# A residual added in SBUF by GpSimd and VectorE instead of by accumulating transfers, at the end of a convolution, attention and recurrence kernel

## The chip, the cores and the metric

The kernel runs on one core of a Trainium2 chip. A core has a matrix engine (TensorE, PE in the profile, with its weight load PEld), three engines for elementwise work (VectorE, DVE; ScalarE, ACT; GpSimd, POOL), an engine that issues transfers (SyncE, SP), and 16 DMA engines which move data between SBUF, the core's memory of 128 partitions, and HBM. PSUM holds the results of matmuls. The metric is device time in microseconds (us) of one execution, as the median of several.

## The reference

The input x has 8 images (B) of 128 channels and 48 x 48 = 2304 tokens. Cut to what matters here:

```python
# layer 0: group norm, then causal attention of each image, added to x
x = x + _L0_conv_ref(_gn(x), Wq, bq, Wk, bk, Wv, bv)
# layer 1
t = _to_tokens(x)
t = t + _L1_attn_ref(_ln_t(t))                      # full attention of the normalized tokens with themselves
t = t + _L1_ffn_ref(_ln_t(t), W, V, gamma, beta)    # the recurrence
x = _from_tokens(t, x)

def _L1_ffn_ref(x, W, V, gamma, beta):
    Wx = jnp.einsum('bti,hi->bth', x, W)
    # ... batch norm of Wx over all images and tokens, gamma and beta
    def step(yt, wx_t):
        yt = jax.nn.sigmoid(wx_t + yt @ V.T)
        return (yt, yt)
    _, ys = jax.lax.scan(step, jnp.zeros((B, H)), jnp.swapaxes(Wx, 0, 1))
    return jnp.swapaxes(ys, 0, 1)
```

The last line of layer 1 matters most: the output is a residual, t after the second attention (t2 in the kernel), plus the states y of the recurrence, for 8 x 2304 tokens of 128 channels: 9.44 MB in fp32.

## The kernel before

The kernel does the two attentions image by image, and keeps W times the normalized tokens in SBUF (wx). When all images are done, and so the statistics of the batch norm are known, the recurrence runs. It isn't done token after token: the 2304 tokens are cut into 96 segments (SEGS) of LS = 24 steps, which run side by side. Each segment begins with 12 warm-up steps (WARM) on the tokens before it. At the end, the last state of each segment is compared with the warmed-up state of the next; a flag says whether they differ too much, and a general path, which isn't taken here, would then compute all again. The 96 segments are in three groups of 32 (SG), so that a step is three matmuls of 256 columns (8 images x 32 segments), one for each group; while one group is in ScalarE another is in TensorE.

The residual is written to the output as soon as the attention has it, group by group of segments:

```python
def keep():                                   # for each image b and chunk j of 384 tokens
    tp = transposed(c["t2"], f"tk_{b}_{j}")
    g, s0 = divmod(j * SJ, SG)
    if s0 == 0:
        self.t2c = work1.tile([P, LS, SG], F32, tag="t2c", name=f"t2c_{b}_{g}")
    nc.scalar.copy(self.t2c[:, :, ds(s0, SJ)], tp[:, :QC].rearrange("p (s l) -> p l s", l=LS))
    if s0 + SJ == SG:
        nc.sync.dma_start(out[g, :, :, b, :], self.t2c)
```

The recurrence adds the states to it with transfers that accumulate, issued by GpSimd, four steps at a time (TO), and two at a time at the end:

```python
WARM = 12
G = SEG_GROUPS                                # 3
TZ = 2
TO = 4
# ... pools: rst[g] with 4 buffers for y, PSUM for z; zeroing of the banks
mv = rc.tile([P, 2], F32, tag="bn_mv", name="bn_mv")
nc.vector.bn_aggr(mv, stats)                  # batch norm: a and c from mv
# ...
def inputs(g, t):                             # z for two steps: SBUF to PSUM, on VectorE
    # ...
    nc.vector.tensor_scalar(z, wx[:, t : t + TZ, :, s0 : s0 + SG], a, c, ALU.mult, ALU.add)
    # ...
for t in range(-WARM, LS):
    s, so = t % TZ, t % TO
    for g in range(G):
        if s == 0 and t + TZ < LS:
            zs[g].append(inputs(g, t + TZ))
        if so == 0:
            y[g] = rst[g].tile([P, TO, B, SG], F32, tag="y", name=f"y_{g}_{t}")
        z = zs[g][0]
        nc.tensor.matmul(z[:, s], vT_f, prev[g], start=False, stop=True, skip_group_check=True)
        to = warm[g] if t == -1 else y[g][:, so]
        nc.scalar.activation(to, z[:, s], AF.Sigmoid)
        prev[g] = to
        # ...
        if so == TO - 1 and 0 <= t < LS - 1:
            nc.gpsimd.dma_start(out[g, :, t + 1 - TO : t + 1], y[g], accum_op=ALU.add)
        if t >= LS - TO and s == TZ - 1:
            nc.gpsimd.dma_start(out[g, :, t + 1 - TZ : t + 1], y[g][:, so + 1 - TZ : so + 1], accum_op=ALU.add)

d = rc.tile([P, G, B, SG], F32, tag="d", name="d")
dm = rc.tile([P, G], F32, tag="dm", name="dm")
for g in range(G):                            # the seams between segments
    n = SG if g < G - 1 else SG - 1
    nc.vector.tensor_sub(d[:, g, :, : SG - 1], prev[g][:, :, : SG - 1], warm[g][:, :, 1:])
    if n == SG:
        nc.vector.tensor_sub(d[:, g, :, SG - 1 :], prev[g][:, :, SG - 1 :], warm[g + 1][:, :, 0:1])
    nc.vector.tensor_reduce(dm[:, g : g + 1], d[:, g, :, :n], AX.XY, ALU.max, apply_absolute_value=True)
# ... off from dm, a matmul over the partitions, and the flag
```

After that every engine loads the flag and branches:

```python
redo = nc.values_load(flag[0:1, 0:1], min_val=0, max_val=1, ...)     # L1359
with tc.If(redo > 0):                                                # L1360
    general_path(tc, *args)
```

GpSimd has one more task in the attention that is used below: it multiplies 128 x 128 blocks of the probabilities by a triangle of ones (L950), while VectorE adds up the probabilities (L971).

Of the kernel before, what the change touches and what calls it, by code (L numbers as in the profile page):

```python
# [13 lines left out]
F32 = mybir.dt.float32  # L14
AF = mybir.ActivationFunctionType
ALU = mybir.AluOpType
AX = mybir.AxisListType
# [7 lines left out]
SEGS = 96  # L25
SEG_GROUPS = 3
# [574 lines left out]
def fast_path(ctx: ExitStack, tc: tile.TileContext, x, wq, bq, wk, bk, wv, bv, w_ffn, v_ffn, gamma, beta, pe, out, flag):  # L601
    nc = tc.nc
    B, C, H, W = x.shape
    N = H * W
    P = 128
    assert C == P and N % P == 0
    NB = N // P
    CH = 512
# [9 lines left out]
    dpool = ctx.enter_context(tc.tile_pool(name="dram", bufs=1, space=DRAM))  # L618


    LS = N // SEGS
    SG = SEGS // SEG_GROUPS
    SJ = QC // LS
    wx = cpool.tile([P, LS, B, SEGS], F32, tag="wx", name="wx")

    posb_d = dpool.tile([P, NQ, 3, QC], F32, tag="posb_d", name="posb_d")

    ident = cpool.tile([P, P], F32, tag="ident", name="ident")
# [20 lines left out]
    with ExitStack() as actx:  # L649
# [40 lines left out]
        def load_x(b):  # L690
# [12 lines left out]
            out=grp3, in_=grp3, compare_op=ALU.is_ge, fill=0.0, base=0, pattern=[[-cg, GROUPS], [0, cg]], channel_multiplier=1  # L703
        )
        nc.gpsimd.affine_select(
            out=grp3, in_=grp3, compare_op=ALU.is_ge, fill=0.0, base=cg - 1, pattern=[[cg, GROUPS], [0, cg]], channel_multiplier=-1
# [323 lines left out]
        class Full:  # L1030
# [103 lines left out]
            def after(self, j, o):  # L1134
                b, rows, tsum = self.b, self.rows, self.tsum
                cols = ts(j, QC)
                c = {}
                o_sb = chunk_tile("o", f"of_{b}_{j}", c, 2)
                nc.scalar.copy(o_sb, o[:, :QC])
                at = st.then(st.now, [("ACT", 0.5)])  # L1140

                def sums():

                    dn = small.tile([P, QB], F32, tag="dn", name=f"dn_{b}_{j}")
                    nc.vector.tensor_reduce(dn, rows[:, QB * j : QB * (j + 1), : j + 1], AX.X, ALU.add)
                    n = NQ - 1 - j
                    if n:
                        tp = psum_t(f"ts_{b}_{j}")
                        k = n * R * QB
                        nc.tensor.matmul(  # L1150
                            tp[:, :k], same.rearrange("p a c -> p (a c)"), tsum[j][:, :n, :].rearrange("p n k -> p (n k)"),
                            start=True, stop=True,
                        )
                        own = small2.tile([P, NQ - 1, R, QB], F32, tag="own", name=f"own_{b}_{j}")
                        nc.vector.tensor_mul(
                            own[:, :n].rearrange("p n a g -> p (n a g)"), tp[:, :k], mine[:, :n].rearrange("p n a g -> p (n a g)")
                        )
                        more = small.tile([P, QB], F32, tag="more", name=f"more_{b}_{j}")
                        nc.vector.tensor_reduce(more, own[:, :n].rearrange("p n a g -> p g (n a)"), AX.X, ALU.add)
                        nc.vector.tensor_add(dn, dn, more)  # L1160
                    ri = small.tile([P, QB], F32, tag="ri", name=f"ri_{b}_{j}")
                    nc.vector.reciprocal(ri, dn)
                    c["ri"] = ri

                def residual():
                    tp = transposed(o_sb, f"of_t_{b}_{j}")
                    t2 = chunk_tile("t2", f"t2_{b}_{j}", c, 5)
                    for g in range(QB):
                        nc.vector.scalar_tensor_tensor(
                            t2[:, ts(g, P)], tp[:, ts(g, P)], c["ri"][:, g : g + 1], t1_tok[b, j][:, ts(g, P)], ALU.mult, ALU.add  # L1170
                        )
                    c["t2"] = t2
                    c["mv"], c["ve"] = moments(t2, f"f{b}_{j}", "l2")

                def rooted():
                    c["rs"] = root(c["ve"], f"f{b}_{j}", "l2")

                def normed():
                    c["x2"] = chunk_tile("x2", f"x2_{b}_{j}", c, 6)
                    normalize(c["x2"], c["t2"], c["mv"], c["rs"])  # L1180

                def keep():
# [4 lines that stand above are left out]
                        self.t2c = work1.tile([P, LS, SG], F32, tag="t2c", name=f"t2c_{b}_{g}")  # L1187
                    nc.scalar.copy(self.t2c[:, :, ds(s0, SJ)], tp[:, :QC].rearrange("p (s l) -> p l s", l=LS))
                    if s0 + SJ == SG:
                        nc.sync.dma_start(out[g, :, :, b, :], self.t2c)  # L1190

                def back():
                    tp = transposed(c["x2"], f"tx_{b}_{j}")
                    c["xc"] = chunk_tile("xc", f"xc_{b}_{j}", c, 7, bufs=1)
                    nc.scalar.copy(c["xc"], tp[:, :QC])

                def statistics():
                    tp = psum_t(f"wx_{b}_{j}")
                    nc.tensor.matmul(tp[:, :QC], w1T, c["xc"], start=True, stop=True)  # L1199
                    nc.vector.bn_stats(stats[:, b * NQ + j, :], tp[:, :QC])  # L1200
                    nc.scalar.copy(wx[:, :, b, ts(j, SJ)], tp[:, :QC].rearrange("p (s l) -> p l s", l=LS))

                c["chain"] = st.add([
                    (sums, 0.15, [("DVE", 0.8)]),
                    (residual, 0.35, [("DVE", 2.6)]),
                    (rooted, 0.0, [("POOL", 0.9)]),
                    (keep, 0.35, [("ACT", 0.5)]),
                    (normed, 0.0, [("DVE", 1.1)]),
                    (back, 0.35, [("ACT", 0.5)]),
                    (statistics, QC * US, [("DVE", 0.55), ("ACT", 0.85)]),  # L1210
                ], max(at, st.free["DVE"]) + 0.2 - st.now)
# [37 lines left out]
    WARM = 12  # L1249
    G = SEG_GROUPS  # L1250
    TZ = 2
    TO = 4
    assert LS * SEGS == N and WARM % TZ == 0 and LS % TO == 0 and SG * B * TZ == CH
    with ExitStack() as rctx:
        rc = rctx.enter_context(tc.tile_pool(name="rconst", bufs=1))
        rst = [rctx.enter_context(tc.tile_pool(name=f"rst{g}", bufs=4)) for g in range(G)]
        ps_z = [rctx.enter_context(tc.tile_pool(name=f"ps_z{g}", bufs=2, space=PSUM)) for g in range(G)]
        ps_w = rctx.enter_context(tc.tile_pool(name="ps_w", bufs=1, space=PSUM))

        rctx.enter_context(tc.manual_schedule())  # L1260

        zero = rc.tile([P, CH], mybir.dt.bfloat16, tag="zero", name="zero")
        nc.gpsimd.memset(zero, 0.0)
# [41 lines left out]
        prev, warm, y = [], [], [None] * G  # L1305
        for g in range(G):
# [3 lines left out]
            warm.append(rc.tile([P, B, SG], F32, tag=f"warm_{g}", name=f"warm_{g}"))  # L1310
            zs[g].append(inputs(g, -WARM))

        for t in range(-WARM, LS):
            s, so = t % TZ, t % TO
            for g in range(G):
                if s == 0 and t + TZ < LS:
                    zs[g].append(inputs(g, t + TZ))
                if so == 0:
                    y[g] = rst[g].tile([P, TO, B, SG], F32, tag="y", name=f"y_{g}_{t}")
                z = zs[g][0]  # L1320
                nc.tensor.matmul(z[:, s], vT_f, prev[g], start=False, stop=True, skip_group_check=True)  # L1321
                to = warm[g] if t == -1 else y[g][:, so]
                nc.scalar.activation(to, z[:, s], AF.Sigmoid)
                prev[g] = to
                if t == -1 and g == 0:
                    nc.vector.memset(warm[0][:, :, 0:1], 0.0)
                if s == TZ - 1:
                    zs[g].popleft()

                if so == TO - 1 and 0 <= t < LS - 1:  # L1330
                    nc.gpsimd.dma_start(out[g, :, t + 1 - TO : t + 1], y[g], accum_op=ALU.add)
                if t >= LS - TO and s == TZ - 1:
                    nc.gpsimd.dma_start(out[g, :, t + 1 - TZ : t + 1], y[g][:, so + 1 - TZ : so + 1], accum_op=ALU.add)

        d = rc.tile([P, G, B, SG], F32, tag="d", name="d")
        dm = rc.tile([P, G], F32, tag="dm", name="dm")
        for g in range(G):
            n = SG if g < G - 1 else SG - 1
            nc.vector.tensor_sub(d[:, g, :, : SG - 1], prev[g][:, :, : SG - 1], warm[g][:, :, 1:])
            if n == SG:  # L1340
                nc.vector.tensor_sub(d[:, g, :, SG - 1 :], prev[g][:, :, SG - 1 :], warm[g + 1][:, :, 0:1])
            nc.vector.tensor_reduce(dm[:, g : g + 1], d[:, g, :, :n], AX.XY, ALU.max, apply_absolute_value=True)
        off = rc.tile([P, 1], F32, tag="off", name="off")
        nc.vector.tensor_reduce(off, dm, AX.X, ALU.max)
        nc.vector.tensor_scalar(off, off, STATE_TOL, None, ALU.is_gt)
# [44 lines left out]
```

## Time and profile before

| | |
|---|---|
| median of 3 runs | 1867.28 us (1866.15 to 1867.42) |
| the profiled execution | 1867.69 us, span of the profile 1866.0 us |
| PE busy | 1817.0 us, 97% of the span |
| DVE, ACT, POOL busy | 65%, 41%, 10% |
| transfers issued by SyncE | 188.79 MB |
| transfers issued by GpSimd (the accumulating ones) | 9.44 MB |

The span is the time from the first to the last instruction of the profiled execution. A line such as L1331 is a line of the kernel's source. The lists of instructions give, for a group, the tile written, the tile read, the shape, and busy time and mean duration in ns. An engine that ends with a q (PEq, POOLq, SPq) is that engine's sequencer, which handles waits, branches and transfers. The chain of waits is followed back from the last instruction: at each step it names what released the next. A table by windows gives the busy time of each engine in chosen stretches of the span, with the granted TensorE clock, the mean busy share of the 16 DMA engines and the GB/s they moved. Kinds of transfer are listed with KB each and the median us from issue to landing.

### The profile page before, as it was taken

Reading aid. Unit: us, or ns where it says so; the run is one execution under the profiler, and the core shown is the slowest. Engines: PE = TensorE matmul, PEld = TensorE weight load, DVE = VectorE, ACT = ScalarE, POOL = GpSimd, SP = SyncE. Lnnn points to the kernel's source line nnn. Section 1 sums busy time; section 2 is a strip of 40 time slices with the busy share of each in tenths; the row PEclk is TensorE's granted clock in tenths of the full one; section 3 lists DMA queues with packets and bytes.
Section 4 is the critical chain, followed back from the end, with each engine's and each line's share of the span. In section 5 each row is a group of like instructions: output and inputs, shape, how many; then the busy total and the mean of one; then the engine's idle time right before and its main releaser. Section 6 shows DMA issues by size and latency. Waiting matters only on the chain.

```text
span 1866.0 us, 22237 instructions
## 1 busy us (share of the span) xinstructions
PE 1817.0 (97%) x6885; PEld 1159.3 (62%) x6886; DVE 1212.5 (65%) x3146; ACT 773.6 (41%) x1976; POOL 187.3 (10%) x288
## 2 busy tenths in 40 slices
PE   7999999999999999999999999999999999999984
PEld 4666666666666666666666666666666666666663
DVE  5747667576766667476676767666675766756473
ACT  2345334443344424453344433444244533444353
POOL 1100011000110002000110001100020001100013
PEclk9999999999999999999999999999999999999987
DMA  2105551256204561055512462045610554024619
GB/s 91 51 1 190 158 129 32 92 158 176 70 14 140 162 160 47 3 188 163 128 28 95 155 180 66 13 140 164 157 47 6 185 163 121 9 71 154 173 24 190
DMA packets 173982, 200.43 MB, mean 107 GB/s; under 512 B 85465, under 2 KB 147548, under 8 KB 173854
## 3 DMA queue, kind: packets, MB, share of 16 engines
q1 hardware_dynamic: 169728, 188.79, 35.3%
q0 software_dynamic: 3024, 9.44, 2.7%
q8 instruction: 57, 0.93, 0.2%
q10 hardware_dynamic: 1102, 0.68, 0.2%
q14 instruction: 71, 0.58, 0.1%
HBM read 105.67 MB, written 93.19 MB: 107 GB/s over the span
## 4 chain that ended last, share of the span: by engine, by line
PE 95%; DMA 2%; issue 1%; DVE 1%; ACT 0%; POOL 0%; SPq 0%; POOLq 0%; DVEq 0%
PE s L1114 18%; PE o L1128 17%; PE s L945 16%; PE o L956 16%; PE o L1124 12%; PE pj L850 3%; PE pj L853 2%; PE wx L1199 2%; PE dn L987 1%; PE x_t L908 1%; PE tb L908 1%; DMA out_dram<-y 1%; PE of_t L908 1%; PE tx L908 1%; PE z L1321 1%
## 5 line engine op out<-in xcount | busy, mean ns | idle before, releaser
L1116 ACT ACTIVATE p<-s,shift 128x384 f32<-128x384 f32 x504 | 293.0, 581 | 448.5 <-PE s L1114 435.5
L1114 PE MATMUL s<-xh 128*128 128x384 f32 x1008 | 410.8, 489 | 0.0
L1128 PE MATMUL o<-p,xhT 128*128 128x384 f32 x1008 | 403.2, 487 | 0.0
L945 PE MATMUL s<-q,k 128*128 128x384 f32 (+2 forms) x1008 | 379.7, 458 | 0.5 <-DVE k L860 0.5
L956 PE MATMUL o<-p,vT 128*128 128x384 f32 (+2 forms) x1008 | 376.9, 456 | 0.0
L947 ACT ACTIVATE p<-s 128x384 f32<-128x384 f32 (+2 forms) x504 | 230.9, 462 | 349.5 <-PE s L945 286.5
L1124 PE MATMUL o<-g,xhT 128*128 128x384 f32 x720 | 279.7, 488 | 0.3 <-DMA g<-e 0.3
L1128 PEld LDWEIGHTS o<-p,xhT 128*128 128x128 f32 x1008 | 188.0, 190 | 121.3
L956 PEld LDWEIGHTS o<-p,vT 128*128 128x128 f32 x1008 | 188.5, 190 | 114.4
L1114 PEld LDWEIGHTS s<-xh 128*128 128x128 f32 x1008 | 183.7, 190 | 106.8
L971 DVE TENSOR_TENSOR acc<-acc,p 128x384 f32<-128x384 f32 (+2 forms) x408 | 210.3, 515 | 59.9 <-ACT p L947 38.0
L945 PEld LDWEIGHTS s<-q,k 128*128 128x128 f32 x1008 | 178.3, 191 | 88.8 <-DVE acc L971 1.1
L1077 DVE STREAM_TRANSPOSE t<-p 128x384 f32<-128x384 f32 x360 | 187.0, 553 | 45.1 <-ACT p L1116 42.5
L1124 PEld LDWEIGHTS o<-g,xhT 128*128 128x128 f32 x720 | 132.1, 190 | 79.3 <-issue 1.5
L1087 DVE TENSOR_REDUCE tsum<-t 128x12 f32<-128x1152 f32 x120 | 162.4, 1353 | 4.1
L855 DVE TENSOR_TENSOR z<-pj,pb 128x384 f32<-128x384 f32 x144 | 79.3, 551 | 110.4 <-PE pj L850 105.6
L950 POOL TENSOR_TENSOR p<-p,triu 128x128 f32<-128x128 f32 x144 | 72.2, 502 | 447.4 <-ACT p L947 446.6
L898 POOL TENSOR_TENSOR rs_f<-ve_f,mhalf 128x3 f32<-128x3 f32 x48 | 41.5, 865 | 687.2 <-DVE ve_f L892 687.2
L1116 ACT ACTIVATION_READ_ACCUMULATOR p<-s,shift 128x1 f32 x504 | 97.3, 193 | 0.0
L989 DVE RECIPROCAL ric<-dn 128x3 f32<-128x3 f32 x48 | 8.5, 177 | 135.9 <-PE dn L987 135.9
L999 DVE SCALAR_TENSOR_TENSOR t1t<-oc_t,ric,xr 128x128 f32<-128x128 f32 x144 | 41.6, 345 | 68.3 <-ACT xr L996 67.9
L850 PE MATMUL pj<-xn,wT 128*128 128x384 f32 x192 | 80.7, 506 | 0.0
(236 smaller groups left out, 1570.6 us busy)
## 6 DMA issues: line engine op xcount, KB each, us to landing
e<-t SPq DMA_DIRECT2D x120, 576.0 KB, 3.3
g<-e SPq DMA_DIRECT2D x480, 144.0 KB, 3.8
pb<-posb_d SPq DMA_DIRECT2D x42, 576.0 KB, 4.2
x<-in_x_dram SPq DMA_DIRECT2D x16, 576.0 KB, 4.7
out_dram<-t2c SPq DMA_DIRECT2D x24, 384.0 KB, 4.4
out_dram<-y POOLq DMA_DIRECT2D x15, 512.0 KB, 13.3
posb_d<-pb SPq DMA_DIRECT2D x6, 576.0 KB, 2.8
out_dram<-y POOLq DMA_DIRECT2D x6, 256.0 KB, 16.5
```

Source lines behind the costliest of these rows:

```text
L850: nc.tensor.matmul(ps[:, :QC], wT[:, j, :], xn, start=True, stop=True)
L855: nc.vector.tensor_add(z, ps[:, :QC], c["pb"][:, j, :])
L945: nc.tensor.matmul(s[:, off:QC], keys[b][:, ts(m, P)], queries[b, j][:, off:], start=True, stop=True)
L947: nc.scalar.activation(p[:, off:], s[:, off:QC], AF.Exp, scale=SCALE)
L956: nc.tensor.matmul(o[:, off:QC], vals[b][:, ts(m, P)], p[:, off:], start=first, stop=last)
L971: nc.vector.tensor_add(a[:, off:], a[:, off:], p[:, off:])
L1077: nc.vector.transpose(t[:, :, :, g, :].rearrange("p b j r -> p j b r"), p.rearrange("p (j b r) -> p j b r", j=QB, b=R))
L1087: nc.vector.tensor_reduce(self.tsum[j][:, n - j - 1, :], t.rearrange("p b j m r -> p (b j) (m r)"), AX.X, ALU.add)
L1114: nc.tensor.matmul(s[:, :QC], xh[:, ts(m, P)], xh[:, ts(j, QC)], start=True, stop=True)
L1116: nc.scalar.activation(p, s[:, :QC], AF.Exp, bias=shift, accum_out=self.rows[:, m, j : j + 1])
L1124: nc.tensor.matmul(out_ap, xhT[:, QB * i + g, :], p, start=first, stop=last)
L1128: nc.tensor.matmul(o[:, :QC], xhT[:, what[1], :], p, start=first, stop=last)
```

## The change

Two thirds of the residual, groups 1 and 2, and the last four steps of group 0, no longer go to the output from the attention but to a scratch tensor in HBM (t2_d). Behind the attention they are loaded into SBUF (t2s). In the recurrence they are added there to the states, two steps at a time: by GpSimd up to step 19, by VectorE for the last four steps. SyncE then stores the sums to the output with plain transfers. The first 20 steps of group 0 are accumulated by transfers as before. The y tiles of groups 1 and 2 hold two steps in place of four and have six buffers in place of four, and the comparison of the seams is done for each group as soon as its last step is there. It is meant to replace transfers that accumulate, which read and write the output, by additions in SBUF and plain stores.

```diff
+    t2_d = dpool.tile([SEG_GROUPS, P, LS, B, SG], F32, tag="t2_d", name="t2_d")
+    LM = LS - 4
@@ keep()
-                        nc.sync.dma_start(out[g, :, :, b, :], self.t2c)
+                        n = 0 if g else LM
+                        if n:
+                            nc.sync.dma_start(out[g, :, :n, b, :], self.t2c[:, :n])
+                        nc.sync.dma_start(t2_d[g, :, n:, b, :], self.t2c[:, n:])
@@ the recurrence
-    TO = 4
+    TO = [4] + [2] * (G - 1)
-        rst = [rctx.enter_context(tc.tile_pool(name=f"rst{g}", bufs=4)) for g in range(G)]
+        rst = [rctx.enter_context(tc.tile_pool(name=f"rst{g}", bufs=4 if g == 0 else 6)) for g in range(G)]
+        t2s = [rc.tile([P, LS if g else LS - LM, B, SG], F32, tag=f"t2s_{g}", name=f"t2s_{g}") for g in range(G)]
+        for l in range(0, LS, 8):
+            for g in range(1, G):
+                nc.sync.dma_start(t2s[g][:, l : l + 8], t2_d[g, :, l : l + 8])
+        nc.sync.dma_start(t2s[0], t2_d[0, :, LM:])
+        def seams(g):
+            # ... the body of the loop over the seams, for one group
@@ in the loop over t and g
-                if so == TO - 1 and 0 <= t < LS - 1:
-                    nc.gpsimd.dma_start(out[g, :, t + 1 - TO : t + 1], y[g], accum_op=ALU.add)
-                if t >= LS - TO and s == TZ - 1:
-                    nc.gpsimd.dma_start(out[g, :, t + 1 - TZ : t + 1], y[g][:, so + 1 - TZ : so + 1], accum_op=ALU.add)
                 if s == TZ - 1:
                     zs[g].popleft()
+                    l0 = t + 1 - TZ
+                    if 0 <= l0 and (g or l0 >= LM):
+                        r = t2s[g][:, l0 : l0 + TZ] if g else t2s[0][:, l0 - LM : l0 - LM + TZ]
+                        (nc.gpsimd if l0 < LM else nc.vector).tensor_add(r, y[g][:, so + 1 - TZ : so + 1], r)
+                        nc.sync.dma_start(out[g, :, l0 : l0 + TZ], r)
+                    elif l0 >= 0 and so == TO[0] - 1:
+                        nc.gpsimd.dma_start(out[0, :, t + 1 - TO[0] : t + 1], y[0], accum_op=ALU.add)
+                if t == LS - 1:
+                    seams(g)
```

More of the change, by code (lines that the diff above doesn't have):

```diff
@@ L1251, in fast_path @@
     TZ = 2
-    TO = 4
-    assert LS * SEGS == N and WARM % TZ == 0 and LS % TO == 0 and SG * B * TZ == CH
+    TO = [4] + [2] * (G - 1)
+    assert LS * SEGS == N and WARM % TZ == 0 and LS % TO[0] == 0 and SG * B * TZ == CH
     with ExitStack() as rctx:
         rc = rctx.enter_context(tc.tile_pool(name="rconst", bufs=1))
-        rst = [rctx.enter_context(tc.tile_pool(name=f"rst{g}", bufs=4)) for g in range(G)]
+        rst = [rctx.enter_context(tc.tile_pool(name=f"rst{g}", bufs=4 if g == 0 else 6)) for g in range(G)]
         ps_z = [rctx.enter_context(tc.tile_pool(name=f"ps_z{g}", bufs=2, space=PSUM)) for g in range(G)]
@@ L1311, in fast_path @@
             zs[g].append(inputs(g, -WARM))
+        d = rc.tile([P, G, B, SG], F32, tag="d", name="d")
+        dm = rc.tile([P, G], F32, tag="dm", name="dm")
+        def seams(g):
+            n = SG if g < G - 1 else SG - 1
+            nc.vector.tensor_sub(d[:, g, :, : SG - 1], prev[g][:, :, : SG - 1], warm[g][:, :, 1:])
+            if n == SG:
+                nc.vector.tensor_sub(d[:, g, :, SG - 1 :], prev[g][:, :, SG - 1 :], warm[g + 1][:, :, 0:1])
+            nc.vector.tensor_reduce(dm[:, g : g + 1], d[:, g, :, :n], AX.XY, ALU.max, apply_absolute_value=True)
         for t in range(-WARM, LS):
-            s, so = t % TZ, t % TO
+            s = t % TZ
             for g in range(G):
@@ L1317, in fast_path @@
                     zs[g].append(inputs(g, t + TZ))
+                so = t % TO[g]
                 if so == 0:
-                    y[g] = rst[g].tile([P, TO, B, SG], F32, tag="y", name=f"y_{g}_{t}")
+                    y[g] = rst[g].tile([P, TO[g], B, SG], F32, tag="y", name=f"y_{g}_{t}")
                 z = zs[g][0]
@@ L1328, in fast_path @@
                     zs[g].popleft()
-                if so == TO - 1 and 0 <= t < LS - 1:
-                    nc.gpsimd.dma_start(out[g, :, t + 1 - TO : t + 1], y[g], accum_op=ALU.add)
-                if t >= LS - TO and s == TZ - 1:
[L1333 to L1342, printed above, removed]
+                    l0 = t + 1 - TZ
[7 more added lines that the diff above has]
+                    seams(g)
         off = rc.tile([P, 1], F32, tag="off", name="off")
```

## The prediction

> **What bounds the kernel now.** I read the windows first, because busy shares of the whole span mix two stages. Up to 1776 us TensorE is busy without a break (attention). From 1791 to 1840 us come 36 steps of three groups each, one matmul every 0.43 us in the chain of waits, again at full TensorE. The rest is tail. Columns below: window, its length, then busy us and (instructions) of PE, PEld, DVE, ACT, POOL, then granted clock, DMA share, GB/s.
>
> ```profile
> core 0: us, PE busy (x) PEld busy (x) DVE busy (x) ACT busy (x) POOL busy (x), PEclk, DMA share, GB/s
> 1812.00:1814.00 2.00, 2.00 (x11) 1.76 (x10) 1.65 (x3) 1.76 (x6) 0.37 (x1) 1.00 0.00 0
> 1814.00:1838.00 24.00, 24.00 (x113) 21.11 (x112) 19.52 (x27) 21.34 (x57) 13.06 (x15) 1.00 1.01 190
> 1838.00:1862.40 24.40, 1.84 (x10) 1.21 (x8) 3.00 (x11) 1.89 (x5) 5.19 (x6) 0.59 1.07 203
> ```
>
> The 16 DMA engines are saturated from the first accumulating transfer (1814) to 1862.4: 9.44 MB in 48.4 us, 195 GB/s. TensorE stops at 1840, so 22 us of the tail are transfers alone. The chain of waits, in order of time (start, us, what), and the page's list of transfers (KB each, us to landing) say the same:
>
> ```profile
> 1834.32 16.75 DMA out_dram<-y
> 1851.07 0.02 issue
> 1851.10 0.02 POOLq L1333
> 1851.11 0.48 issue
> 1851.59 0.88 POOLq L1359
> ```
> ```profile
> out_dram<-y POOLq DMA_DIRECT2D x15, 512.0 KB, 13.3
> out_dram<-y POOLq DMA_DIRECT2D x6, 256.0 KB, 16.5
> ```
>
> Under the transfers lies a second floor: the end of the program. The flag is written at 1842.7; each engine then loads it and branches.
>
> ```profile
> L1359 PEldq TENSOR_LOAD <-flag x1: 1771/1771/1771, 1842.7 to 1842.7; - x1
> L1359 POOLq TENSOR_LOAD <-flag x1: 1488/1488/1488, 1851.6 to 1851.6; - x1
> ```
> ```profile
> L1360 PEldq COMPARE_BRANCH  x1: 6777/6777/6777, 1844.6 to 1844.6; - x1
> L1360 POOLq COMPARE_BRANCH  x1: 45/45/45, 1853.1 to 1853.1; - x1
> L1360 POOLq EVENT_SEMAPHORE  x1: 17/17/17, 1859.7 to 1859.7; - x1
> ```
>
> The branch costs 6.8 us on PE (1844.6 to 1851.4) and 6.6 on POOL (1853.1 to 1859.7), which arrives last because its accumulating issues held it until 1851.6. So even with no transfers at all the end would be 1842.7 + 1.8 + 6.8 + about 2 of closing waits = 1853.3: at most 13 us of the 22 can be had.
>
> **What the Trainium skill says.** (1) "GPSIMD Engine Reference", section 3, gives a GpSimd tensor_tensor add over 2048 fp32 as 4497 ns and calls it about twice VectorE's. The trace has GpSimd's 128x128 product at 457 ns median (the mean, 502, holds the delays of (2)); a line through both is 457 + 384 x 2.1 = 1.27 us for 128x512, an estimate; no run here shows that size yet. (2) "SBUF — State Buffer", "Who interferes with whom": a VectorE instruction with two SBUF inputs excludes a GpSimd one that reads SBUF; one with at most one SBUF input outside the 2-port modes doesn't. The trace agrees with the first half: the product doubles beside a VectorE add and is 0.45 us alone.
>
> ```profile
> 44.10 0.91 POOL L950 TENSOR_TENSOR p<-p,triu 128x128 f32<-128x128 f32 x1 [2.24 <-ACT p L947]
> 44.15 0.55 DVE L971 TENSOR_TENSOR acc<-acc,p 128x384 f32<-128x384 f32 x1
> ...
> 45.96 0.45 POOL L950 TENSOR_TENSOR p<-p,triu 128x128 f32<-128x128 f32 x1 [0.95 <-ACT p L947]
> ```
>
> (3) "VectorE: DVE Perf Modes", "Why PSUM operands drop a tier": with a PSUM operand the 2-port mode is out. The recurrence's z (SBUF to PSUM, 0.81 us each) should so leave GpSimd alone; GpSimd reads no SBUF operand beside it in this trace, so that isn't shown. (4) "DMA: Bandwidth & Descriptors", "Measured", gives 341 GB/s for a 1 MB load; in the trace the first load of x (4.6 KB pieces) runs at 417 GB/s, in the window from 4 to 6 us.
>
> **The change, part by part.**
> Attention: the instruction order on PE, DVE and ACT is the same but for buffer names up to the recurrence, and GpSimd and SyncE differ only in where t2c is stored: 24 stores become 32 of the same bytes. 0 us.
>
> Loads: 6 of 1.05 MB and one of 0.52 MB, 6.8 MB, in 8 KB pieces. In the built program the first waits for the last use of the attention's tiles (the residual, 1779.2 us) and the others for the last store of t2c (issued 1780.1, landed about 1785). At 340 to 417 GB/s the remaining 5.8 MB need 14 to 17 us: done by 1803. The first add comes at step 1, about 1811.4. The DMA is idle from 1784 to 1814 now, so this is hidden: 0 us.
>
> GpSimd in the recurrence: two steps last 6 x 0.432 = 2.59 us. Per two steps it now has 2 adds of 1.27 and half an accumulating issue of 0.88: 2.98 us. It falls behind by 0.4 us each time. From 1811.4: 20 x 1.27 + 5 x 0.88 + 1 us of gaps = 30.8, so it would end at 1842.2, against 1835 if it kept up. Ring: y of groups 1 and 2 has 6 buffers of two steps, so a step waits for the add of twelve steps before; that bites only above about 4.3 us per two steps. The recurrence stays at TensorE's pace and still ends at 1840.2.
>
> VectorE at the end: six adds at 0.68 us (558 ns for 384 elements in the trace, 325 for 128: 0.9 per element), 4.1 us, and the seam checks, which moved among them. Without interference: first adds at 1836.8, then the last group's step at 1840.2, flag at about 1845.3 (1842.7 before). But GpSimd is adding until after 1842, and two-input adds exclude one another: four GpSimd adds (5.1 us) interleave with VectorE's. I take a third to a half of that on VectorE's chain: flag 1847; GpSimd, delayed by three VectorE adds, ends about 1845.
>
> Transfers: the accumulating ones fall from 9.44 MB to 2.62 MB (13 us at 205 GB/s), the plain stores are 6.8 MB (20 us at 340). 33 us of work lie between 1813 and 1850, so there's no long backlog. SyncE stores in order: the last six stores stand behind GpSimd's last add (1845); 8 x 0.26 MB at 340 GB/s are 6 us, landing 2 us later: 1853.
>
> Sum: flag 1847 + load 1.8 + branch 5 to 6.8 (the branch was timed while the DMA was saturated; I don't know how much of it that is) + 2 of closing = 1856 to 1857.6. The transfers' 1853 and their wait of 1.7 us at the end are just below. Span 1856.7; the median before is 1.3 us above its span: **1858 us**, 9.3 us less, half a per cent.
>
> **The rivals.**
> GpSimd becomes the bound. If an add costs 1.9 us instead of 1.27, GpSimd ends at 1811.4 + 38 + 5.4 = 1854.8, then 1.5 + 6.6 + 1.5 for its flag, branch and close: 1864.4, or 1866 as a time, nearly nothing gained. For it: the average of the 144 products is 502 ns, above the median, and GpSimd is already short of time by my sum. Against: 4497 ns for 2048 elements leaves little room.
>
> z and GpSimd exclude each other after all. Then per two steps 2.43 us of z and 2.54 + 0.44 of GpSimd are in series, 5.4 us in place of 2.59, and the recurrence's last 24 steps take 65 us instead of 31: about 1890. Against: the issues of accumulating transfers (2.6 us for three) cost as much beside z as after it. They don't read SBUF operands, so this is weak evidence, but with (3) I give it 4 in 100.
>
> The exclusion at the end costs nothing and the branch shrinks once the DMA is quiet: flag 1845.3 + 1.8 + 4 + 2 = 1853, time 1854. For it: the page shows DMA share 1.07 during PE's branch. One in five.
>
> Stores slower than thought: at 210 GB/s (as the accumulating ones) the last stores end at 1857 and set the end, 1860.
>
> **Range and chances.** The floor of 1853 forbids 2% (37 us) of gain, unless the branch vanished; only the second rival makes 2% of loss. The middle cases lie between 1854 and 1866. Range 1850 to 1866; faster 0.01, same 0.96, slower 0.03.
>
> **What would show it.** Right: loads landed before 1806; GpSimd's adds near 1.27 us and busy almost without gaps from 1811 to 1845; PE busy until 1840; in the chain of waits the end belongs to the flag and the branch, not to out_dram<-y; DMA share well under 1 after 1850. Wrong: adds of 1.9 us or more, ACT waiting for GpSimd's adds in the recurrence, z above 0.81 us, VectorE adds longer than 0.7 us by waiting (then the exclusion is larger than I took), or a last store that lands after the branch.

## The result and the profile after

| | before | after |
|---|---|---|
| median | 1867.35 us (1866.15 to 1869.34) | **1855.2 us** (1853.79 to 1856.92) |
| ratio, 95% interval | | 0.9934 [0.9917, 0.9952] |
| the profile's span | 1866.0 us | 1852.4 us |
| start of the last recurrence matmul | 1839.3 us | 1838.6 us |
| from there to the end (the tail) | 26.7 us | 13.8 us |

The change takes 12 us, two thirds of a per cent. From execution to execution the mean granted clock differs in the third digit (0.986 to 0.995 in these runs), and the end of the attention moves with it by several us. So where a few us matter, I read each profile from the start of TensorE's last recurrence matmul on. That stretch is called the tail below.

First the windows of the changed kernel, with the columns of the prediction's windows:

```profile
1796.00:1800.00 4.00, 4.00 (x21) 3.51 (x20) 3.86 (x7) 3.57 (x10) 0.00 (x0) 1.00 1.01 426
1800.00:1804.00 4.00, 4.00 (x20) 3.54 (x19) 3.91 (x7) 3.56 (x10) 0.00 (x0) 1.00 0.33 129
...
1814.00:1838.00 24.00, 24.00 (x113) 20.91 (x112) 20.86 (x28) 21.26 (x56) 24.00 (x23) 1.00 1.03 262
...
1844.00:1846.00 2.00, 0.19 (x2) 0.09 (x2) 1.61 (x6) 0.00 (x0) 0.00 (x0) 0.50 1.06 408
1846.00:1848.00 2.00, 0.00 (x0) 0.00 (x0) 0.17 (x1) 0.00 (x0) 0.00 (x0) 0.50 0.63 223
1848.00:1850.00 2.00, 0.00 (x0) 0.00 (x0) 0.00 (x0) 0.00 (x0) 0.00 (x0) 0.50 0.02 8
```

The loads run at 426 GB/s; a DMA share of 0.33 in the second window puts their end near 1801.5, well ahead of the first add (1810.56). TensorE is as busy as before in 1814 to 1838, and GpSimd now without a gap (24.00 against 13.06). The transfers are over by 1848, not 1862. The page's list of transfers (KB each, us to landing) has the plain ones that took over:

```profile
out_dram<-t2s SPq DMA_DIRECT2D x26, 256.0 KB, 3.9
...
t2s<-t_d SPq DMA_DIRECT2D x6, 1024.0 KB, 6.9
```

A store lands 3.9 us after its issue; the accumulating transfers of before took 13.3 and 16.5. Next GpSimd's timeline (start, us, engine, line, what) and the list of the z instructions (ns min/median/max):

```profile
1810.56 2.50 POOL L1358 TENSOR_TENSOR t2s<-y,t2s 128x512 f32<-128x512 f32 x2 [21.52 <-ACT y L1348]
...
1813.79 5.25 POOL L1358 TENSOR_TENSOR t2s<-y,t2s 128x512 f32<-128x512 f32 x4
1818.69 1.19 POOL L1361 DMA_DIRECT2D out_dram<-y  x1
1819.30 5.55 POOL L1358 TENSOR_TENSOR t2s<-y,t2s 128x512 f32<-128x512 f32 x4
...
1835.86 4.59 POOL L1358 TENSOR_TENSOR t2s<-y,t2s 128x512 f32<-128x512 f32 x2
```
```profile
L1308 DVE TENSOR_SCALAR z<-wx,bn_a,bn_c x36: 802/805/816, 1804.9 to 1834.8; 128x512 f32<-128x512 f32 x36
```

Read the starts, not the durations: GpSimd's records overlap (20 adds at a median of 2.02 us would be 40 us, and the engine was busy with them for 28.9), but four adds and an issue take 1819.30 - 1813.79 = 5.51 us. Of that the adds have 4.90, 1.23 us each, and the issue 0.61. Four steps of TensorE last 5.18, so GpSimd falls behind by 0.33 us each time and ends at 1835.86 + 4.59 = 1840.45. The z instructions, which run beside it the whole time, keep their 0.805 us.

VectorE's timeline at the end:

```profile
1835.98 5.63 DVE L1358 TENSOR_TENSOR t2s<-y,t2s 128x512 f32<-128x512 f32 x4 [0.35 <-ACT y L1348]
...
1842.39 0.68 DVE L1358 TENSOR_TENSOR t2s<-y,t2s 128x512 f32<-128x512 f32 x1
...
1845.97 0.21 DVE L1369 TENSOR_SCALAR flag<-pw,fl 1x1 int32<-1x1 f32 x1 [0.28 <-PE pw L1368]
```

Alone an add takes 0.68 us. The first four, which lie beside GpSimd's last two, take 5.63 us in place of 2.7. The chain of waits runs through them to the flag, and no transfer stands between the last additions and the flag, whereas 16.75 us of one stood ahead of GpSimd's flag load before:

```profile
1837.60 4.01 DVE t2s L1358 x3
...
1845.97 0.21 DVE flag L1369
```

Then PE loads the flag and branches:

```profile
L1381 PEldq TENSOR_LOAD <-flag x1: 554/554/554, 1846.2 to 1846.2; - x1
```
```profile
L1382 PEldq COMPARE_BRANCH  x1: 4437/4437/4437, 1846.9 to 1846.9; - x1
L1382 PEldq EVENT_SEMAPHORE  x1: 51/51/51, 1851.4 to 1851.4; - x1
```

Load 0.55 (1.77 before), branch 4.44 (6.78 before), and 1.0 from 1851.4 to the end. Before, GpSimd's close was much longer: the first of its drains behind the branch took 5.38 us, beside accumulating transfers that were still in flight. The list of the last line's instructions, of the kernel before and of the changed one:

```profile
L1386 POOLq DRAIN  x3: 44/107/5382, 1859.8 to 1865.7; - x3
```
```profile
L1408 POOLq DRAIN  x3: 44/107/474, 1850.6 to 1852.2; - x3
```

So the tail adds up on both sides. Before: 3.4 (flag) + 8.9 (GpSimd held until 1851.6 by its issues, which waited for earlier transfers to land) + 1.5 (its load) + 6.6 (its branch) + 6.3 (drain and close) = 26.7. After: 7.6 + 0.55 + 4.44 + 1.05, and 0.15 between them, = 13.8. The flag gave back 4.2 us of the 17.1 that left the other terms.

### The profile page after: what moved, and what is told of

The parts are those of the page before. It is cut to its first block, busy times and chain, and to the rows that moved or that the text cites. A ratio compares the mean times of both kernels' runs of the same rounds, so it can differ in the third digit from the quotient of the medians.

```text
span 1852.4 us, 22328 instructions
## 1 busy us (share of the span) xinstructions
PE 1817.4 (98%) x6885; PEld 1159.6 (63%) x6886; DVE 1218.8 (66%) x3152; ACT 773.5 (42%) x1976; POOL 198.4 (11%) x292
## 4 chain that ended last, share of the span: by engine, by line
PE 96%; DVE 1%; POOL 1%; DMA 1%; issue 1%; ACT 0%; SPq 0%; POOLq 0%; DVEq 0%
PE s L1117 18%; PE o L1131 18%; PE s L948 16%; PE o L959 16%; PE o L1127 13%; PE pj L853 3%; PE pj L856 2%; PE wx L1205 2%; PE dn L990 1%; PE x_t L911 1%; PE tb L911 1%; PE of_t L911 1%; PE tx L911 1%; PE oc_t L911 1%; PE z L1346 1%; PE tk L911 1%
```

## The experiments

**The theory (A)**: behind the recurrence, flag, load and branch set the end, and load and branch are longer while the DMA engines are busy. I supposed that this is because the instructions behind a branch come through the same DMA engines; that part isn't shown. **The main rival (C)**: the last bytes to land set the end, however the flag stands. The table has each kernel's tail, all in us; "flag" is from the start of the last recurrence matmul until PE can load it. Tail, flag, load and branch are of the one execution that was profiled. A ratio is to executions of the kernel before taken beside it; their medians were 1867.4 us, and 1869.5 beside e9 to e11.

| kernel | median | ratio, 95% | tail | flag | PE load | PE branch |
|---|---|---|---|---|---|---|
| before | 1867.4 | | 26.7 | 3.4 | 1.77 | 6.78 |
| after | 1855.2 | 0.9934 [0.9917, 0.9952] | 13.8 | 7.6 | 0.55 | 4.44 |
| after again (e9) | 1855.2 | 0.9933 [0.9918, 0.9947] | 13.6 | 7.6 | 0.49 | 4.29 |
| e1 no accumulating transfers | 1851.3 | 0.9912 [0.9896, 0.9928] | 9.6 | 3.4 | 0.50 | 4.49 |
| e2 no adds | 1850.9 | 0.9912 [0.9896, 0.9927] | 10.1 | 3.5 | 0.91 | 4.40 |
| e3 last four steps accumulated | 1857.3 | 0.9946 [0.993, 0.9962] | 17.8 | 4.6 | 1.56 | 7.22 |
| e4 flag ahead of the last adds | 1855.6 | 0.9936 [0.992, 0.9951] | 15.1 | 5.9 | 0.49 | 4.44 |
| e5 plain stores beside the branch | 1855.4 | 0.9937 [0.9923, 0.9951] | 15.9 | 3.5 | 1.11 | 6.04 |
| e6 GpSimd done early | 1854.8 | 0.9933 [0.9918, 0.9949] | 12.2 | 5.2 | 0.80 | 4.95 |
| e6 again (e11) | 1853.1 | 0.9912 [0.9897, 0.9926] | 12.4 | 5.2 | 0.79 | 5.13 |
| e7 last six on VectorE | 1856.2 | 0.993 [0.9914, 0.9946] | 12.8 | 4.3 | 0.93 | 4.92 |
| e8 and last stores from ScalarE | 1852.4 | 0.9916 [0.9902, 0.9931] | 12.6 | 4.2 | 0.90 | 4.41 |
| e8 again (e10) | 1855.9 | 0.9933 [0.9919, 0.9946] | 13.3 | 4.3 | 1.23 | 5.04 |

**e1: the kernel before without its 21 accumulating transfers.** The states are left out of the output; this is the floor, which I had put at 1853.3 us of span.

```diff
-                if so == TO - 1 and 0 <= t < LS - 1:
-                    nc.gpsimd.dma_start(out[g, :, t + 1 - TO : t + 1], y[g], accum_op=ALU.add)
-                if t >= LS - TO and s == TZ - 1:
-                    nc.gpsimd.dma_start(out[g, :, t + 1 - TZ : t + 1], y[g][:, so + 1 - TZ : so + 1], accum_op=ALU.add)
```

> The kernel before, with its 21 accumulating transfers left out: the output is the residual alone, without the states. What is left behind the recurrence is the flag, its load, the branch and the close. Theory A (load and branch are slow in the kernel before because the DMA is saturated, and with a quiet DMA they take 0.55 and 4.4 us as in the changed kernel): the flag stands at 1842.7 as before, PE's branch takes 4.4 us, span 1849, time 1850 to 1851. Theory B (flag load 1.8 and branch 6.8 us belong to this program whatever the DMA does): span 1853, time 1854 to 1855. If the accumulating transfers were no bound at all the time would stay at 1867.

The flag comes as early as before (3.4), and load and branch shrink. The lists of the two lines' instructions:

```profile
L1355 PEldq TENSOR_LOAD <-flag x1: 495/495/495, 1842.7 to 1842.7; - x1
```
```profile
L1356 PEldq COMPARE_BRANCH  x1: 4493/4493/4493, 1843.3 to 1843.3; - x1
```

What the DMA engines carry from 1843.3 to 1848, during that branch (queue, packets, MB, share), is instructions alone:

```profile
q14 instruction: 8, 0.07, 4.9%
q8 instruction: 1, 0.02, 2.0%
```

So 1.3 us of the load and 2.3 of the branch came from transfers beside them. The floor is a span of 1848.9 and a median of 1851.3, 4 us under the changed kernel. That the branch waits for these packets is an inference from their place in time; that it is longer when the engines are busy for the whole of it is shown, here and by e5. Where they are busy for a part only, no rule comes out: in e8 the stores ran at 403 GB/s for the first 2.6 us of PE's branch and it took 4.41 us, in its repeat e10 they ran at 399 GB/s for as long, and it took 5.04.

**e2: the changed kernel without its 26 adds.** The states are stored without the residual, which is loaded but not added.

```diff
-                        (nc.gpsimd if l0 < LM else nc.vector).tensor_add(r, y[g][:, so + 1 - TZ : so + 1], r)
-                        nc.sync.dma_start(out[g, :, l0 : l0 + TZ], r)
+                        nc.sync.dma_start(out[g, :, l0 : l0 + TZ], y[g][:, so + 1 - TZ : so + 1])
```

> The changed kernel with its 26 additions left out: loads, plain stores and the five accumulating transfers stay, but the stores take the states as they are, so the residual is missing from two thirds of the output and from the last four steps of group 0. Theory A (the changed kernel's end is set by the flag, which the six VectorE additions and their exclusion with GpSimd's hold back by 3 to 4 us): flag at about 1842, time 3 to 4 us below the changed kernel's 1855.2, so 1851 to 1852. Theory C (the plain stores and the saturated DMA, share about 1.05 from 1816 on, set the end): they start a little earlier without the additions, but the time stays within 1 us of 1855.2, and the last store lands after the branch.

The flag is back at 3.5 and the tail at 10.1, half a us above e1. With the same transfers as in the changed kernel, the adds are thus what costs it 3.7 us of tail (4.3 in the medians), by the flag alone: 7.6 - 3.5 = 4.1, less a load that is 0.36 longer. The intervals of the ratios of e1, e2 and the changed kernel overlap, as the clock differs between executions. But those with the same recorded clock, 0.993, lie apart: 1854.15 for the changed kernel (one execution), 1850.6 and 1851.3 for e1, 1850.2 to 1851.0 for e2.

**e3: the last four steps by accumulating transfers**, as in the kernel before; the last four steps' residual goes straight to the output, the other adds stay on GpSimd.

```diff
@@ keep() and the loads: steps 20 to 23 go to out, and only groups 1 and 2 are loaded
@@ the recurrence
-                    if 0 <= l0 and (g or l0 >= LM):
-                        r = t2s[g][:, l0 : l0 + TZ] if g else t2s[0][:, l0 - LM : l0 - LM + TZ]
-                        (nc.gpsimd if l0 < LM else nc.vector).tensor_add(r, y[g][:, so + 1 - TZ : so + 1], r)
+                    if l0 >= LM:
+                        nc.gpsimd.dma_start(out[g, :, l0 : l0 + TZ], y[g][:, so + 1 - TZ : so + 1], accum_op=ALU.add)
+                    elif 0 <= l0 and g:
+                        r = t2s[g][:, l0 : l0 + TZ]
+                        nc.gpsimd.tensor_add(r, y[g][:, so + 1 - TZ : so + 1], r)
                         nc.sync.dma_start(out[g, :, l0 : l0 + TZ], r)
```

> The changed kernel with one part undone: the last four steps of all groups are again added by accumulating transfers (six of 256 KB), none by VectorE. Flag at about 1842.5, as VectorE has only the seams. Theory A: the six transfers are issued behind GpSimd's additions, from about 1841 on, 0.9 us apart if the rings let them, 1.6 MB at 205 GB/s are 8 us; they land at about 1851, GpSimd reaches its flag load at 1846 to 1850, and its own branch of 4.4 to 6.6 us follows: time 1857 to 1861, so 2 to 6 us above the changed kernel's. Theory D (VectorE's additions are a cost and the accumulating transfers of the last four steps would hide beside the branch): time 1852, 3 us below.

The flag comes 3 us earlier than in the changed kernel, and the end 4 us later in the tail (2.1 in the medians): load and branch are back at 1.56 and 7.22 and GpSimd drains again. The list of the last line's instructions:

```profile
L1409 POOLq DRAIN  x3: 44/107/3759, 1857.7 to 1862.2; - x3
```

The profiled execution of e3 had a low clock (0.988); its one execution at 0.993 took 1857.45 us, against the changed kernel's 1854.15. The VectorE adds at the end therefore pay for themselves: what they cost on the flag is less than what six accumulating transfers cost behind it.

**e4: the changed kernel with the flag ahead of the last three adds.** Nothing is left out.

```diff
+                        if l0 < LS - TZ:
                             (nc.gpsimd if l0 < LM else nc.vector).tensor_add(r, y[g][:, so + 1 - TZ : so + 1], r)
                             nc.sync.dma_start(out[g, :, l0 : l0 + TZ], r)
+                        else:
+                            last.append((g, l0, r, y[g][:, so + 1 - TZ : so + 1]))
@@ behind the flag
+        for g, l0, r, ys in last:
+            nc.vector.tensor_add(r, ys, r)
+            nc.sync.dma_start(out[g, :, l0 : l0 + TZ], r)
```

> The changed kernel with VectorE's order changed at the end: the comparison of the seams and the flag come ahead of the last three additions (steps 22 and 23), whose stores come behind. Nothing is left out. Theory A: the flag moves from 1846.2 to about 1844, the branch runs beside the three additions and their stores, which land by about 1848.5: time 2 us below the changed kernel's, 1853. Theory C (stores set the end): the last three stores come 1 to 2 us later than in the changed kernel, so the time rises by 1 to 2 us to 1857.

A miss of theory A: the flag is 1.7 us earlier, PE's branch is over at 1848.6, and yet the median is the same and the tail 1.3 us longer. SyncE is now last: its third store takes 2.18 us to issue (0.33 as a rule), so that it loads the flag only at 1847.5 and ends its branch at 1851.1. Two lists of instructions:

```profile
L1376 SPq DMA_DIRECT2D out_dram<-t2s x3: 332/332/2180, 1844.0 to 1845.3; - x3
```
```profile
L1388 SPq TENSOR_LOAD <-flag x1: 552/552/552, 1847.5 to 1847.5; - x1
```

With an issue of 0.33 us it would have come there at about 1845.7 (an estimate), still 2 us behind the others. So A has to be widened: each engine has its own flag load and branch, and the last engine to reach them sets the end. In the changed kernel SyncE begins its last issue at 1844.6, 1.6 us ahead of the flag:

```profile
L1359 SPq DMA_DIRECT2D out_dram<-t2s x26: 332/332/862, 1811.9 to 1844.6; - x26
```

Why e4's third issue takes 2.18 us isn't shown. It lies beside the other engines' branches, but in e7 one before 1845, ahead of them, took 1.70 us, so the branches alone aren't the reason.

**e5: e1 with eight plain stores of 512 KB** to a scratch tensor, issued by SyncE as soon as group 0 has its last step. Plain traffic stands where accumulating traffic stood.

```diff
+    dump = dpool.tile([8, P, 1024], F32, tag="dump", name="dump")
+    wxf = wx.rearrange("p l b s -> p (l b s)")
+                if t == LS - 1 and g == 0:
+                    nc.vector.tensor_copy(wx[:, 0, 0, 0:1], to[:, 0, 0:1])
+                    for i in range(8):
+                        nc.sync.dma_start(dump[i], wxf[:, i * 1024 : (i + 1) * 1024])
```

> The first experiment again (the kernel before without its accumulating transfers), plus eight plain stores of 512 KB to a scratch tensor, let go when group 0's last step is done: the DMA is busy from about 1840 to 1850 at 400 GB/s, and the flag (about 1842.8) is loaded and branched on in the middle of it. Theory A (a busy DMA stretches load and branch): load over 1.2 us in place of 0.5, PE's branch 6 to 7 us in place of 4.5, time 3 to 4 us above the first experiment's 1851.3. Theory A2 (only accumulating transfers do it, as the second experiment's 0.9 and 4.4 us beside plain stores hint): load under 1 us, branch at 4.5, and the time is set by the last store, which lands at about 1850: 1852 to 1853.

The lists of PE's load and branch, and the window of the branch's first four us:

```profile
L1362 PEldq TENSOR_LOAD <-flag x1: 1107/1107/1107, 1841.3 to 1841.3; - x1
```
```profile
L1363 PEldq COMPARE_BRANCH  x1: 6037/6037/6037, 1842.5 to 1842.5; - x1
```
```profile
1842.00:1846.00 4.00, 0.00 (x0) 0.00 (x0) 0.00 (x0) 0.00 (x0) 0.00 (x0) 0.50 1.05 398
```

Full DMA engines alone lengthen the branch by 1.5 us and the load by 0.6, so it isn't only the accumulating kind that does it; under accumulating ones it was 2.3 to 2.7 and 1.1 to 1.3. The median rises by 4.1 us over e1 and the tail by 6.3. PE's load and branch are 2.2 of that; the rest is SyncE, which is held by its issues (1.2 us each in the median), loads the flag only at 1846.3 and is the last to come out of the branch, at 1852.4.

**e6: the changed kernel without GpSimd's adds of steps 14 to 19** in groups 1 and 2, so that GpSimd is done before VectorE begins. For these steps the states are stored without the residual. (The expectation of the repeat, e11, has it the other way round; the kernel is the same.)

```diff
-                        (nc.gpsimd if l0 < LM else nc.vector).tensor_add(r, y[g][:, so + 1 - TZ : so + 1], r)
+                        if g and LM - 6 <= l0 < LM:
+                            r = y[g][:, so + 1 - TZ : so + 1]
+                        else:
+                            (nc.gpsimd if l0 < LM else nc.vector).tensor_add(r, y[g][:, so + 1 - TZ : so + 1], r)
```

> The changed kernel with GpSimd's additions of steps 14 to 19 left out (six of 20; these states are stored without their residual), so that GpSimd isn't adding when VectorE adds the last four steps. Theory A (two-input adds on the two engines exclude one another, and VectorE's first four adds took 5.6 us in place of 2.7 through it): each VectorE add takes 0.68 us as stamped, the flag comes 2 to 3 us earlier after the recurrence, time 2 to 3 us below the changed kernel's 1855.2. If VectorE's long adds had another cause (the DMA, or the waits for ScalarE), they'd stay at 1.2 us in the median and the time at 1855.

The list of VectorE's adds (679/1187/1747 in the changed kernel):

```profile
L1361 DVE TENSOR_TENSOR t2s<-y,t2s x6: 681/684/693, 1837.3 to 1842.8; 128x512 f32<-128x512 f32 x6
```

All six take 0.68 us and the flag comes 7.6 - 5.2 = 2.4 us earlier: that is the whole cost of the exclusion on the flag. But the median fell by 0.4 us, not by 2 to 3, and the tail by 1.6: the earlier flag meets the stores, and load and branch are 0.25 and 0.5 us longer. As this median and the changed kernel's were taken at different times, e11 ran it again beside the changed kernel.

**e7: VectorE adds the last six steps' worth of groups 1 and 2** (two steps taken from GpSimd), once it has no more z to make, and the last three adds go behind the flag. Nothing is left out.

```diff
+        held = []
+        def add(queue):
+            while held:
+                g, l0, r, ys = held.pop(0)
+                nc.vector.tensor_add(r, ys, r)
+                queue.dma_start(out[g, :, l0 : l0 + TZ], r)
@@ in place of the add and the store of every l0
+                        ys = y[g][:, so + 1 - TZ : so + 1]
+                        if l0 < LM - TZ:
+                            nc.gpsimd.tensor_add(r, ys, r)
+                            nc.sync.dma_start(out[g, :, l0 : l0 + TZ], r)
+                        else:
+                            held.append((g, l0, r, ys))
@@
+                    if t == LS - TZ - 1 and g == G - 1:
+                        add(nc.sync)
@@ behind the flag
+        add(nc.sync)
```

> A version that leaves nothing out: VectorE adds the last six steps of groups 1 and 2 (held until its z work is done), GpSimd the first 18, and the seams and the flag come ahead of the last three adds. Theory A: GpSimd has no backlog left when VectorE begins, five adds take 3.3 to 4.3 us from the end of z, the flag comes 3 us earlier after the recurrence than in the changed kernel (3.8 in place of 7 us after TensorE's last matmul); the last store is issued about 2.5 us after the flag and lands about when PE's branch ends: time 1852 to 1853. If the stores set the end as in the fourth experiment, 1854 to 1855.

Most of the exclusion is gone (five adds in 3.91 us, where five of 0.68 are 3.4) and the flag at 4.3, but SyncE issues its last store at 1848.5, 6 us behind the last matmul, and loads the flag at 1848.9, two us behind the others: as in e4. The tail is 12.8, the median no better than the changed kernel's.

**e8: e7 with the last three stores on ScalarE's queue**, which is idle by then.

```diff
-        add(nc.sync)
+        add(nc.scalar)
```

> The seventh experiment with the last three stores issued by ScalarE's queue instead of SyncE's. In the fourth experiment SyncE took 2.18 us to issue the last store, in place of 0.33. If that lies in SyncE's queue, ScalarE's issues take 0.33 us each and the last store lands 2 us earlier than there: time 1851.5 to 1852.5. If any issue beside the branches of the other engines takes so long, ScalarE's last issue takes 1 to 2 us too, and the time is that of the seventh experiment.

The list of these stores' issues:

```profile
L1344 ACTq DMA_DIRECT2D out_dram<-t2s x3: 338/350/359, 1843.0 to 1844.2; - x3
```

None of these three is late; of SyncE's five ahead of the flag the longest took 1.44 us. The first median was 1852.4. It was taken at another time than the changed kernel's 1855.2, so both ran again on one chip.

**e9, e10, e11: the changed kernel, e8 and e6 again, side by side.**

> The changed kernel itself, beside the two that follow, because the earlier calls had different clocks. The same as before: 1855 us, within 1.5.

> The version with the last six adds on VectorE, the flag ahead of the last three and their stores on ScalarE's queue. Theory A (behind the recurrence the flag, its load and the branch set the end, once no store is issued late) expects 1852.5, 2.5 to 3 us under the changed kernel. Theory C (the last bytes set the end whoever issues them) expects no difference, 1855.

> The changed kernel without GpSimd's adds of steps 14 to 19 (their residual is stored without the states). Theory A (GpSimd's adds, by excluding VectorE's, put the flag 2 to 3 us later) expects 1852.5 to 1853. If the flag comes earlier and the time doesn't, the stores are the bound in the changed kernel as well: 1855.

Measured: 1855.2, 1855.9 and 1853.1 us, with intervals of the ratios that overlap. The gain of e8 **isn't confirmed**: its five executions ran from 1852.88 to 1858.28 us, with the mean clock from 0.993 down to 0.989, and the first 1852.4 was of executions at 0.993 and 0.994. In the tail e8 saves 0.3 to 1.2 us over the changed kernel, as its earlier flag (by 3.3 us) is eaten by a longer load, in e10 by a longer branch too, and by ScalarE, which comes to its flag load 2.1 to 2.2 us behind the others, after its stores. For e6 the tail is 12.4 against 13.6, again half of the flag's 2.4. Executions with the recorded clock of 0.993 hint at a small gain all the same: 1852.4 to 1852.9 for e8 and e10 and 1852.1 to 1853.5 for e6 and e11, against 1854.15. But a step of 0.001 in the clock goes with about 1.4 us (5.4 us over 0.004 in e10), so one such execution of the changed kernel is no proof. No version here beats it by an amount that the runs show; e1 and e2 bound what is left at 4 us.

## Why the prediction was right, and which terms were off

The sum had the right terms and the right bound: the flag, its load, the branch and the close. It gave a gain of 9.3 us, and 12.2 were measured. The range of 1850 to 1866 us was wider than the gain, and the outcomes of all rivals but the second lie in it.

**Attention, 0 us; loads hidden; recurrence at TensorE's pace.** Right. The loads ended near 1801.5 (I said 1803), TensorE shows 24.00 of 24 us in the recurrence, and ScalarE never waits for a ring buffer.

**GpSimd.** Right in kind: 1.27 us was worked out from the Trainium skill's "GPSIMD Engine Reference", section 3, and a trace row; the shortest add of the changed kernel took 1.269, and in a run of them it is 1.23. The lag is 0.33 us per four steps, not 0.8, of which the issue's 0.61 in place of 0.88 makes 0.27 and the adds' 1.23 in place of 1.27 makes 0.18. It began at 1810.56 and ended at 1840.45; I had 1811.4 and 1842.2, or 1845 with the exclusion. The rival in which adds take 1.9 us is out, though my own sign for it (adds of 1.9 us or more) would have misled: the recorded median is 2.02, by overlap.

**z and GpSimd don't exclude each other, two-input adds do.** Both halves of what the Trainium skill, "SBUF — State Buffer", "Who interferes with whom", says are now shown: z 0.805 us beside unbroken adds, VectorE's adds at 0.68 us without GpSimd's (e6) and up to 1.75 beside them. The rival of 1890 us is out.

**The flag.** I had 1847, that is 7.7 us behind the last matmul of before's profile; measured 7.6. That is luck, as two errors cancelled in it. Without interference I had 6.0, and e6 shows 5.2; for the exclusion I took 1.7, and e6 shows 2.4.

**Load, branch and close: the mis-sized term.** I had 1.8 + 5 to 6.8 + 2 = 8.8 to 10.6 us from flag to end, and wrote that I didn't know how much of the branch was due to the saturated DMA. Measured: 0.55 + 4.44 + 1.05 and gaps = 6.2, and 6.0 in e9. That is 3.5 us of the 4.3 by which the span came below my 1856.7; the rest is mostly the recurrence, which ended 0.7 us earlier in that profile. (The median came only 2.8 us below my 1858, because the profiled execution, of 1854.15 us, was one of the two faster of four.) e1 and e5 say why: I carried over a load and a branch that had been timed on full DMA engines. The rival of 1854 us named the branch's half rightly (4 us against 4.4) and was wrong on the exclusion. Its number was nearer than mine because its errors offset each other: its flag was 1.6 us too early, its load and close together 2.2 too long.

**Transfers.** Right in that they don't set the end, wrong in size: plain stores run at 408 GB/s in the tail, and the last landing is before 1848 and not at 1853, 4 us ahead of the end. What lies just below is not the landing but SyncE's last issue: where the flag is earlier and the last stores are later (e4, e7), that issue takes the flag's place. I hadn't seen GpSimd's drain at all. It was 5.4 us of the end of the kernel before; since it goes with the accumulating transfers (5.38 and 3.76 us with them at the end, 0.47 with the last one 15 us before), my sum for the changed kernel didn't need it. The floor of 1853.3 was 4.4 us too high (e1: 1848.9) for the same reason as the load and the branch above: so 17 us could be had, and not 13.

## What to carry to other kernels

When the last transfers are saturated, time the end of the program anew: flag loads, branches and drains that were measured beside them shrink with them (here GpSimd's 1.5 + 6.6 + 6.3 us before to PE's 0.55 + 4.4 + 1.0 after). Moving a sum from the transfers to engines puts the last additions onto the chain that ends the program (4.2 of 17.1 us came back, 2.4 of them by the exclusion), and to shorten that chain alone brings little where the stores end within 2 us of it. Every engine has to come to the branch: the last store's issuer counts like the flag.

## What the runs showed of the hardware beyond that

- A branch to the end of the program took PE 4.3 to 4.5 us on DMA engines that were quiet for most of it (e1, the changed kernel, e9), 4.4 to 5.1 where stores ran beside a larger part of it (e2, e4, e6 to e8, e10, e11), 6.0 beside plain stores at 398 GB/s and 6.8 to 7.2 beside accumulating transfers; loading the flag took PE 0.5 us in e1, 1.1 in e5 and 1.6 to 1.8 beside accumulating transfers.
- After accumulating transfers GpSimd's drain took 3.8 to 5.4 us, 0.5 in the changed kernel, whose last one was issued 15 us before, and at most 0.08 in e1, which has none. It ended 1.4 us (the kernel before) and 1.7 us (e3) behind the last packet of the accumulating queue.
- Single SyncE store issues in the tail took 2.18 us (e4, beside the other engines' branches) and 1.70 (e7, before them), and 1.44 and 1.63 (e8 and e10, ahead of the flag), against 0.33; ScalarE's took 0.34 to 0.36 in the tail of e8.
